# Two layers in one launch: the layer-1 projections without GpSimd products, and half of W_down's products moved behind the last expert pair

## The chip, the cores and the metric

The kernel runs on one core of one Trainium2 chip, in one launch. The metric is the device time of that core in microseconds. TensorE is called PE here, its weight loads PEld, VectorE DVE, ScalarE ACT, GpSimd POOL, and SyncE, which issues most of the transfers, SP.

## The reference

The program computes two transformer layers over 2048 tokens of width 512, all in 32-bit floats. Each layer is: a modulated normalization, attention, a residual sum with a gate, a second modulated normalization, a feed-forward part, and a second residual sum with a gate.

- Layer 0: 16 heads with windows of 64 tokens. Its feed-forward part sends each token to 8 of 64 experts (inner width 192), with weights renormalized over the 8.
- Layer 1: queries, keys and values are projections `x @ Wq + bq`, `x @ Wkv + bkv` (16 query heads, 4 key heads). Queries and keys are rotated by position, `x * cos + rotate_half(x) * sin`. The attention sees 16 first tokens and a window of 128.
- The feed-forward part of layer 1, cut to what matters:

```python
x = fwht(x * SU_ug) / SCALE
x_up = x @ W_up.T * (Wscale_ug[:INTER] * SCALE)
x_gate = x @ W_gate.T * (Wscale_ug[INTER:] * SCALE)
x = jax.nn.silu(x_gate) * x_up
x = fwht(x * SU_dp) / SCALE
x = x @ W_down.T * (Wscale_dp * SCALE)
```

`fwht` is a Walsh-Hadamard transform. The one in front of `W_down` is linear, so the kernel applies it to `W_down` instead of to the activations.

## The kernel before

The tokens lie in 16 tiles of 128 rows, in `x_sb`. The stages follow each other: layer-0 attention with the routing, the expert pairs, the layer-1 projections, the layer-1 attention, the layer-1 feed-forward part.

**Expert pairs** (1019 to 1032 us is the last of them). The 64 experts, sorted by load, are served two at a time, in 32 turns `q`. SP fetches an expert's weights two turns ahead (`fetch_w`, tiles `w1` and `w2`, four buffers each). POOL gathers the token rows and later adds the results `yo` into six arrays `sums[0..5]` in DRAM with indirect transfers; turns from 21 on add into the last three only. From turn 22 on, the first three arrays are loaded back (`earlier`, tiles `sa`) and added to `x_sb` on DVE. After the pairs comes a hardware loop `tc.For_i(0, n_more, 1)` for tokens that found no room; here it runs zero times, but all engines meet before it.

**W_down beside the pairs.** `beside()` is a generator that takes two steps in each turn. For each of four column blocks `cb` it loads a block of `W_down` (`wd_load`, tile `wda`), runs four butterfly steps over it on DVE between `wda` and `wdb` (`wd_step`, L992 and L993), multiplies by the 128x128 Hadamard matrix on PE (`wdh`, four products per block), scales the result from PSUM by `ws_dp` on DVE (L1001), and writes the block to `wd_d` in DRAM. The feed-forward part loads `wd_d` after the attention.

**Layer-1 projections** (1040 to 1199 us). The tiles go in five groups, `GROUPS`, of 2, 2, 4, 4 and 4. `prepare(g)` returns steps and a function `across`. A step is `summed(i)` of one tile and `normal(i - 1)` of the tile before: three sums of `x_sb` with the last three arrays (`rest(i)`, loaded by SP; L1155), statistics, a square root on ACT (L1204), then the normalized tile `xn` on DVE. `across` transposes the `xn` tiles of a group on PE (`nT`, L1220) and writes the scaled `hT`.

While group `g` goes through its five matrices (`c` from -1 to 3: the keys, then four blocks of queries), DVE does one step of group `g + 1` per matrix. For each matrix PE makes eight weight passes. DVE makes `by_sin` from PSUM (sum with the bias, product with sin). ACT makes `by_cos` from PSUM and POOL multiplies it by cos (L1274). PE turns `by_sin` by a permutation matrix (`rot`) and DVE adds `by_cos` to that. Behind the group the value matrix `v` is made, and POOL adds the output bias of the attention, `bo1`, to the group's tiles (L1304); behind group 2 it also scales `wo` (L1307). `v_` and `mm_` issue each instruction behind the one before on its engine; the other instructions are placed by a scheduler that orders each engine's queue.

**Layer-1 attention.** For each tile POOL copies a window of keys (`kw`), PE makes scores, DVE masks them, ACT takes exponents, and PE makes values and the output.

Of the kernel before, what the change touches and what calls it, by code (L numbers as in the profile page):

```python
# [12 lines left out]
F32 = mybir.dt.float32  # L13
# [3 lines left out]
AF = mybir.ActivationFunctionType  # L17
# [111 lines left out]
def block_kernel(ctx: ExitStack, tc: tile.TileContext, t: dict, out: bass.AP):  # L129
# [720 lines left out]


    ex = served.enter_context(tc.tile_pool(name="ex", bufs=4))
    with tc.tile_pool(name="h1", bufs=1) as h1, tc.tile_pool(name="p_x", bufs=2, space=PSUM) as p_x, tc.tile_pool(
        name="p_g", bufs=3, space=PSUM
    ) as p_g, tc.tile_pool(name="p_y", bufs=3, space=PSUM) as p_y:

        def fetch_x(r):
            st_[r]["xg"] = []
# [92 lines left out]
        def earlier(n):  # L951

            got = []
            for i in (2 * n, 2 * n + 1):
                for k in range(3):
                    j, at = divmod(3 * i + k, 4)
                    if at == 0:
                        tag, bufs = ("wdb", 1) if j % 3 == 2 else ("wda", 2)
                        st_["sa"] = h1.tile([P, 4, D], F32, tag=tag, name=f"sa_{j}", bufs=bufs)
                    part = st_["sa"][:, at, :]  # L960
                    nc.sync.dma_start(out=part, in_=sums[k][i * P : (i + 1) * P, :])
                    got.append((i, part))
            return got
# [13 lines left out]
            V.tensor_scalar(ws_dp, ws_dp, 1.0 / math.sqrt(INTER), None, ALU.mult)  # L977

        def wd_load(cb):
            a = h1.tile([P, FC, P], F32, tag="wda", name=f"wda_{cb}", bufs=2)  # L980
            nc.sync.dma_start(out=a, in_=t["L1_Wdown"][cb])
            return a

        def wd_step(cb, a):

            b = h1.tile([P, FC, P], F32, tag="wdb", name=f"wdb_{cb}")
            src, dst = a, b
            h = 1
            while h < FC:
                x = src.rearrange("p (n two h) m -> p n two (h m)", two=2, h=h)  # L990
                y = dst.rearrange("p (n two h) m -> p n two (h m)", two=2, h=h)
                V.tensor_tensor(y[:, :, 0, :], x[:, :, 0, :], x[:, :, 1, :], ALU.add)  # L992
                V.tensor_tensor(y[:, :, 1, :], x[:, :, 0, :], x[:, :, 1, :], ALU.subtract)  # L993
                src, dst = dst, src
                h *= 2
                yield
            for c4 in range(0, FC, 4):
                ps = p_x.tile([P, 4, P], F32, tag="xp", name=f"wdh_{cb}_{c4}")
                with in_turn():
                    st_["pe"] = mm(ps, had, src[:, c4 : c4 + 4, :])  # L1000
                V.tensor_tensor(dst[:, c4 : c4 + 4, :], ps, bc(ws_dp[:, cb * P : (cb + 1) * P], 1, 4), ALU.mult)  # L1001
                if c4 == 4:
                    yield
            nc.sync.dma_start(out=wd_d[cb], in_=dst)
# [13 lines left out]
                yield  # L1018

        side = beside()  # L1020
        NQ = len(ROOM)

        def turn(q):

            steps = []
            for r in (2 * q, 2 * q + 1):
                st_[r]["xT"], chunk = x_T(r, st_[r]["xg"], ROOM[q])
                steps += [lambda f=chunk, c=c: f(c) for c in range(KC)]
            return steps
# [23 lines left out]
        for q in range(NQ):  # L1053
            if q == NQ - 1:
                n_more = nc.values_load(more[0:1, 0:1], min_val=0, max_val=MORE)
            two = [st_[2 * q], st_[2 * q + 1]]
            late = st_.pop("late", [])
            if LATE < q <= LATE + NT // 2:
                st_["late"] = earlier(q - LATE - 1)

            def fetch(p):
                for r in (2 * p, 2 * p + 1) if p < NQ else ():
                    fetch_w(r)
                    fetch_x(r)

            if q:
                fetch(q + 2)
            steps = turn(q + 1) if q + 1 < NQ else []
            with in_turn():
                hA, hB, last = gate_up(  # L1070
                    q, [s["w"][0] for s in two], [s["xT"] for s in two], ROOM[q], lambda: take(steps, 2),
                    lambda: take(opening, KC),
                )
            if q == 0:
                fetch(2)
            take(steps, 2)
            if q + 1 < NQ:
                with tc.issue_after(last.ins):
                    shares(q + 1)
            for s in range(0, ROOM[q], P):  # L1080

                with in_turn(), tc.issue_after(st_["gx"].ins):
                    down(q, s, [a["w"][1] for a in two], hA, hB, ROOM[q], [a["share"] for a in two], to_sums(q))
                take(steps, 2)
            take(steps, 2 * KC)
            with tc.issue_after(last.ins):
                for _ in range(2):
                    next(side)
                for i, part in late:
                    V.tensor_tensor(x_sb[:, i, :], x_sb[:, i, :], part, ALU.add)  # L1090


        with tc.For_i(0, n_more, 1) as j:
# [42 lines left out]
    with tc.tile_pool(name="a1", bufs=1) as ap:  # L1136
# [4 lines left out]
        va = ap.tile([P, NT, P], F32, tag="va", name="va")  # L1141
        vs = ap.tile([P, NT, P], F32, tag="vs", name="vs")
        v2 = ap.tile([80, NT, 2, P], F32, tag="v2", name="v2")
        with tc.tile_pool(name="b1", bufs=1) as bp, tc.tile_pool(name="b1h", bufs=2) as hp, tc.tile_pool(
            name="b1n", bufs=5
        ) as np_, tc.tile_pool(name="cb", bufs=3) as cb, tc.tile_pool(name="b1ps", bufs=8, space=PSUM) as psA:

            prev = {}
# [4 lines left out]
            def v_(f, *a):  # L1153
                with after("V"):
                    prev["V"] = f(*a)  # L1155
# [22 lines left out]

            rest(0, nc.scalar)
            rest(1, nc.scalar)  # L1180
            wk = load(bp, "L1_Wk", [P, KC, P])
            wq = load(bp, "L1_Wq", [P, KC, D], nc.scalar)
            angle(0)
            rest(2)
            wv = load(bp, "L1_Wv", [P, KC, P])
            wo = load(ap, "L1_Wo", [P, KC, D])
            hTs = {}

            def prepare(g):
# [17 lines left out]
                def normal(i):  # L1207
                    mv, rs = norms[i]
                    v_(V.reciprocal, rs, rs)
                    xn = np_.tile([P, D], F32, tag="xn", name=f"xn_a1_{i}")  # L1210
                    v_(V.tensor_scalar, xn, x_sb[:, i, :], mv[:, 0, 0:1], rs[:, 0:1], ALU.subtract, ALU.mult)
                    norms[i] = xn

                def across():
# [27 lines left out]
            for step in steps:  # L1242
                step()
            across()
            for g, (first, n) in enumerate(GROUPS):
                w_ = n * P
                cols = slice(first * P, first * P + w_)
                cos, sin = angles[g]
                hT = hTs[g]
                steps, across = [], None  # L1250
                if g + 1 < len(GROUPS):
                    angle(g + 1)
                    steps, across = prepare(g + 1)
                waiting = []

                def turned():
# [7 lines left out]
                for c in range(-1, KC):  # L1264
                    ps = psA.tile([P, D], F32, tag="ps", name=f"q1_{g}_{c}")[:, 0:w_]
                    for k in range(KC):
                        w = wk[:, k, :] if c < 0 else wq[:, k, c * P : (c + 1) * P]
                        mm_(ps, w, hT[:, k, 0:w_], k == 0, k == KC - 1)
                    bias = bk if c < 0 else bq[:, c : c + 1]
                    by_sin = np_.tile([P, D], F32, tag="by_sin", name=f"by_sin_{g}_{c}", bufs=2)[:, 0:w_]  # L1270
                    v_(V.scalar_tensor_tensor, by_sin, ps, bias, sin, ALU.add, ALU.mult)
                    by_cos = np_.tile([P, D], F32, tag="by_cos", name=f"by_cos_{g}_{c}", bufs=3)[:, 0:w_]
                    S.activation(by_cos, ps, AF.Identity, bias=bias)
                    prev["G"] = G.tensor_tensor(by_cos, by_cos, cos, ALU.mult)  # L1274
                    add = turned() if waiting else None
                    if steps:
                        steps.pop(0)()
                    if add:
                        add()
                    waiting.append((c, by_cos, by_sin))  # L1280
# [17 lines left out]
                if g == 0:  # L1298
                    nc.sync.dma_start(
                        out=v2[64:80, :, :, :].rearrange("p i a m -> p (i a) m"), in_=bc(va[0:16, 0, :], 1, 2 * NT)  # L1300
                    )
                with after("G"):
                    for i in range(first, first + n):
                        G.tensor_tensor(x_sb[:, i, :], x_sb[:, i, :], bo1, ALU.add)  # L1304
                    if g == 2:
                        for k in range(KC):
                            G.tensor_tensor(wo[:, k, :], wo[:, k, :], m1[2], ALU.mult)  # L1307


        fx = ctx.enter_context(tc.tile_pool(name="fx", bufs=1, side="right"))  # L1310
        with tc.tile_pool(name="s1", bufs=2) as sp, tc.tile_pool(name="q_s", bufs=4, space=PSUM) as p_s, tc.tile_pool(
# [20 lines left out]
            def scores(i, cp):  # L1332
# [1 line left out]

                nk = P if i == 0 else W + 16
                mask = con(("mask0", "mask1", "mask2")[min(i, 2)])
                if i > 0 and cp == 0:
                    keys[i] = window(i)
                if cp == 0:
                    totals[i] = small.tile([P, 4, 4], F32, tag="tot", name=f"tot_{i}")  # L1340
                for c in (2 * cp, 2 * cp + 1):
# [399 lines left out]
```

## Time and profile before

| what | value |
|---|---|
| median of 3 runs | 2061.43 us (2055.21 to 2065.03) |
| profiled execution, its own time | 2055.3 us |
| its span, first to last instruction | 2053.5 us |
| mean granted clock of TensorE | 0.972 |
| PE busy | 1943.5 us (95%) |
| DVE busy | 1082.3 us (53%) |
| POOL busy | 589.6 us (29%) |
| ACT busy | 511.1 us (25%) |
| last product of the pairs starts, first transpose of layer 1 starts | 1031 us, 1053.4 us |
| first matrix of groups 0, 1, 2, 3, 4 starts | 1055.6, 1076.1, 1102.4, 1137.8, 1172.6 us |
| first scores of the layer-1 attention | 1199.3 us |

Times inside the table's last three rows are counted from the span's start. A share of busy time is an average over stages with different limits, so each stage is read by itself: in the windows of the profile, in the timeline, and in what ended an engine's idle time (given in brackets behind an instruction, as "idle before" and the releaser). Engines name the line of the kernel; where a helper issues the instruction, as at L134 and L1155, the names of the tiles tell what it is.

### The profile page before, as it was taken

To read this page: it belongs to the slowest core of one execution; us is meant where nothing else is said; L and a number is where in the kernel's file an instruction comes from. 1 tells how busy PE (TensorE), PEld (TensorE's weight loads), DVE (VectorE), ACT (ScalarE), POOL (GpSimd) and SP (SyncE) were. 2 spreads that over 40 slices of the span, in tenths; PEclk is the share of its full clock that TensorE was granted. 3 is DMA by queue.
4 is the path that set the end of the run, shared out by engine and by line. 5 is a ranking of instruction groups with operands and counts; after the bars stand their busy time and mean duration, and the time that the engine had idled before them with its cause. 6 is when DMAs were issued, how large, how long until landed. Compare 5 with 4: busy or idle time off the path is not lost. (4 is left out here: it accounts for less than half of the span.)

```text
span 2053.5 us, 28795 instructions
## 1 busy us (share of the span) xinstructions
PE 1943.5 (95%) x10794; PEld 1245.2 (61%) x10794; DVE 1082.3 (53%) x2566; ACT 511.1 (25%) x1190; POOL 589.6 (29%) x463
## 2 busy tenths in 40 slices
PE   8999878999999999999957889999999999999998
PEld 4655545455555556666634555556776777767776
DVE  3566564544444433345548657766545535545443
ACT  2333323111111111111111157774111111111101
POOL 1500003576666766566522420020010010010000
PEclk9999968999999999999979899999999999999999
DMA  7780036688888899999964100002211211211210
GB/s 281 293 329 22 32 113 206 156 213 233 208 233 221 225 245 241 267 319 314 270 195 146 48 12 2 2 23 95 91 62 42 83 44 59 82 42 62 83 41 21
DMA packets 121166, 290.31 MB, mean 141 GB/s; under 512 B 20968, under 2 KB 28904, under 8 KB 118464
## 3 DMA queue, kind: packets, MB, share of 16 engines
q1 hardware_dynamic: 83552, 207.13, 29.3%
q0 software_dynamic: 36032, 77.30, 17.8%
q10 hardware_dynamic: 1440, 4.00, 0.5%
q8 instruction: 87, 1.43, 0.3%
q14 instruction: 55, 0.45, 0.1%
HBM read 209.92 MB, written 76.10 MB: 139 GB/s over the span
## 5 line engine op out<-in xcount | busy, mean ns | idle before, releaser
L934 POOL DMA_INDIRECT sum<-yo,tidx x164 | 269.9, 1646 | 108.8 <-issue 39.2
L608 POOL DMA_INDIRECT xring<-h_d,tidx x164 | 180.4, 1100 | 377.6 <-PE rps L134 232.3
L134 PE MATMUL gu<-xT,w 128*128 128x312 f32 (+26 forms) x1024 | 244.4, 397 | 0.0
L134 PE MATMUL y<-wd,act 128*128 128x512 f32 x512 | 230.3, 593 | 1.5 <-DVE act L1510 1.4
L134 PEld LDWEIGHTS gu<-xT,w 128*128 128x128 f32 x1024 | 190.2, 191 | 54.5 <-issue 17.3
L134 PEld LDWEIGHTS y<-wd,act 128*128 128x128 f32 x512 | 97.0, 190 | 98.0 <-issue 91.4
L876 ACT ACTIVATE xT<-xp,modc,modc 128x312 f32<-128x312 f32 (+26 forms) x128 | 74.2, 580 | 329.5 <-PE xp L873 302.9
L930 DVE SCALAR_TENSOR_TENSOR yo<-y,wc,modr 128x512 f32<-128x512 f32 (+22 forms) x164 | 116.6, 745 | 74.5 <-PE y L134 74.1
L134 PE MATMUL y<-w,hA 128*128 128x512 f32 (+22 forms) x328 | 149.8, 596 | 1.1 <-DVE yo L930 1.0
L237 POOL TENSOR_TENSOR xh<-hT 128x1024 f32<-128x1024 f32 x4 | 9.4, 2359 | 418.0 <-ACT hT L1585 402.8
L896 DVE TENSOR_TENSOR hA<-hA,gu 128x312 f32<-128x312 f32 (+26 forms) x64 | 28.2, 440 | 188.1 <-PE xp L873 107.9
L134 PE MATMUL p<-xt,ws 128*128 128x256 f32 x512 | 122.6, 383 | 3.5 <-DVE ws L1510 3.5
L134 PE MATMUL gub<-xT,w 128*64 128x312 f32 (+26 forms) x1024 | 125.4, 398 | 0.0
L134 PE MATMUL p<-xt,wr 128*128 128x256 f32 x512 | 120.8, 379 | 0.0
L1371 ACT ACTIVATE pr<-ng,nb 128x208 f32<-128x208 f32 (+1 forms) x256 | 115.0, 450 | 22.8 <-DVE nb L1361 22.8
L873 PEld LDWEIGHTS xp<-cst,xring 128*128 128x128 f32 x656 | 73.1, 143 | 73.0 <-issue 57.9
L134 PE MATMUL p<-xh,wr 128*128 128x256 f32 x512 | 116.5, 379 | 0.0
L134 PEld LDWEIGHTS p<-xt,ws 128*128 128x128 f32 x512 | 97.9, 192 | 27.9 <-issue 15.8
L134 PEld LDWEIGHTS p<-xt,wr 128*128 128x128 f32 x512 | 96.8, 190 | 23.6 <-issue 10.8
L873 PE MATMUL xp<-cst,xring 128*128 128x128 f32 x656 | 100.2, 284 | 6.1 <-DMA xring<-h_d,tidx 4.9
L134 PEld LDWEIGHTS p<-xh,wr 128*128 128x128 f32 x512 | 97.0, 190 | 13.6 <-issue 0.7
L1665 ACT ACTIVATE sg<-two,L_ws_gate 128x512 f32<-128x512 f32 x32 | 23.1, 722 | 309.0 <-DVE two L1510 309.0
(378 smaller groups left out, 2992.4 us busy)
## 6 DMA issues: line engine op xcount, KB each, us to landing
w<-in_L_gu SPq DMA_DIRECT2D x64, 768.0 KB, 7.5
wr<-in_L_Wug SPq DMA_DIRECT2D x64, 512.0 KB, 4.5
sum<-xring SPq DMA_DIRECT2D x6, 4352.0 KB, 30.9
w<-in_L_dn SPq DMA_DIRECT2D x64, 256.0 KB, 8.7
sa<-sum SPq DMA_DIRECT2D x48, 256.0 KB, 10.5
sum<-sum SPq DMA_DIRECT2D x44, 256.0 KB, 3.3
w<-in_L_dn SPq DMA_DIRECT2D x64, 128.0 KB, 9.1
xring<-in_L_wmod SPq DMA_DIRECT2D x4, 1536.0 KB, 11.0
```

Source lines behind the costliest of these rows:

```text
L134: return TE.matmul(o, lhsT, rhs, start=start, stop=stop)
L237: eng.tensor_tensor(b[:, :, 0, :], a[:, :, 0, :], a[:, :, 1, :], ALU.add)
L608: return G.indirect_dma_start(out=dst, out_offset=None, in_=src[:, :], in_offset=bass.IndirectOffsetOnAxis(ap=idx, axis=0))
L873: st_["pe"] = TE.transpose(xp[:, b * P : (b + 1) * P], xg[:, c * P : (c + 1) * P], ident)
L876: S.activation(xT[:, c, 0:n], xp[:, 0:n], AF.Identity, bias=sh, scale=sc)
L896: V.tensor_tensor(o[:, 0:n], o[:, 0:n], ps[1][:, 0:n], ALU.mult)
L930: V.scalar_tensor_tensor(yo, ys[h], shares[h][rows, b : b + 1], m0[5][rows, :], ALU.mult, ALU.mult)
L934: G.indirect_dma_start(out=sums[k][:, :], out_offset=bass.IndirectOffsetOnAxis(ap=idx, axis=0), in_=yo, in_offset=None, compute_op=ALU.add,)
L1371: S.activation(prs[i, c][:, j, :nk], ng[:, :nk], AF.Exp, bias=nb, scale=-1.0, accum_out=totals[i][:, c, j : j + 1],)
L1665: S.activation(sg, gate, AF.Silu, scale=wsg[:, f : f + 1])
```

## The change

1. **W_down.** For the column blocks 2 and 3, DVE scales the block by `ws_dp` in SBUF behind the butterflies, and the block goes to `wd_d` without the Hadamard product. In the last turn these blocks are loaded again in eight pieces, into buffers of expert weights (`fetch_last`). Behind the last pair PE makes the eight products, ACT and DVE copy them out by turns, and ACT and SP write them back to `wd_d` (`last_products`).
2. **Weights.** `Wk`, `Wq`, `Wv` and the first group's cos and sin are loaded in the last turn (`load_proj`) into two `wda` buffers, which move to a pool of their own that stays open through the projections.
3. **Projections.** `by_cos` is made by one DVE instruction from PSUM, with the bias and cos, as `by_sin` is. `xn` is made by ACT, with a small `off` from DVE. The bias adds of `x_sb` and the scaling of `wo` stand in the source of the attention now, still on POOL.
4. **Order.** `prepare(g + 2)` is called behind group `g`, and its first step (the sums of the first tile) is done there.

The diff, cut to its core:

```diff
+    h2 = early.enter_context(tc.tile_pool(name="h2", bufs=2, side="right"))
+    def load_proj():
+        a, b = (h2.tile([P, 4 * D], F32, tag="wda", name=f"proj_{i}") for i in range(2))
+        at = 0
+        for key, w, n in (("L1_Wk", b, P), ("L1_Wq", a, D), ("L1_Wv", b, P)):
+            lo = at if w is b else 0
+            proj[key] = w[:, lo : lo + KC * n].rearrange("p (k m) -> p k m", k=KC)
+            nc.sync.dma_start(out=proj[key], in_=t[key])
+            at += KC * n if w is b else 0
+        proj["angle"] = [b[:, at + 2 * P * k : at + 2 * P * (k + 1)] for k in range(2)]
+        for k in range(2):
+            nc.sync.dma_start(out=proj["angle"][k], in_=t["rope"][k][:, 0 : 2 * P])
...
+            if cb >= 2:
+                for c8 in (0, 8):
+                    part = src[:, c8 : c8 + 8, :]
+                    V.tensor_tensor(part, part, bc(ws_dp[:, cb * P : (cb + 1) * P], 1, 8), ALU.mult)
+                    yield
+                nc.sync.dma_start(out=wd_d[cb], in_=src)
+                yield
+                return
...
+        def fetch_last():
+            parts = [(cb, c4) for cb in (2, 3) for c4 in range(0, FC, 4)]
+            got = []
+            for tag, n in (("w1", 3), ("w2", 2), ("w1", 3)):
+                a = ew.tile([P, KC, 2 * FI] if tag == "w1" else [P, 2, D], F32, tag=tag, name=f"wdl_{len(got)}")
+                a = a.rearrange("p k f -> p (k f)").rearrange("p (g c m) -> p g c m", c=4, m=P)
+                for g in range(n):
+                    cb, c4 = parts[len(got)]
+                    nc.sync.dma_start(out=a[:, g], in_=wd_d[cb][:, c4 : c4 + 4, :])
+                    got.append((cb, c4, a[:, g]))
+            return got
+        def last_products(got):
+            for n, (cb, c4, a) in enumerate(got):
+                ps = p_x.tile([P, 4, P], F32, tag="xp", name=f"wdh_{cb}_{c4}")
+                with in_turn():
+                    st_["pe"] = mm(ps, had, a)
+                o = ex.tile([P, D], F32, tag="yo", name=f"wdo_{n}", bufs=8).rearrange("p (c m) -> p c m", c=4)
+                (V.tensor_copy if n % 2 else S.copy)(o, ps)
+                (nc.sync if n % 2 else nc.scalar).dma_start(out=wd_d[cb][:, c4 : c4 + 4, :], in_=o)
...
+            if q == NQ - 1:
+                load_proj()
+                behind_it = fetch_last()
...
+        last_products(behind_it)
         with tc.For_i(0, n_more, 1) as j:
...
+                    off = small.tile([P, 1], F32, tag="off", name=f"off_a1_{i}")
+                    v_(V.scalar_tensor_tensor, off, mv[:, 0, 0:1], -1.0, rs, ALU.mult, ALU.mult)
                     xn = np_.tile([P, D], F32, tag="xn", name=f"xn_a1_{i}")
-                    v_(V.tensor_scalar, xn, x_sb[:, i, :], mv[:, 0, 0:1], rs[:, 0:1], ALU.subtract, ALU.mult)
+                    S.activation(xn, x_sb[:, i, :], AF.Identity, bias=off, scale=rs)
...
-                    S.activation(by_cos, ps, AF.Identity, bias=bias)
-                    prev["G"] = G.tensor_tensor(by_cos, by_cos, cos, ALU.mult)
+                    v_(V.scalar_tensor_tensor, by_cos, ps, bias, cos, ALU.add, ALU.mult)
...
-                with after("G"):
-                    for i in range(first, first + n):
-                        G.tensor_tensor(x_sb[:, i, :], x_sb[:, i, :], bo1, ALU.add)
-                    if g == 2:
-                        for k in range(KC):
-                            G.tensor_tensor(wo[:, k, :], wo[:, k, :], m1[2], ALU.mult)
+                made = [], None
+                if g + 2 < len(GROUPS):
+                    angle(g + 2)
+                    made = prepare(g + 2)
+                    made[0].pop(0)()
...
-                if i > 0 and cp == 0:
-                    keys[i] = window(i)
+                if cp == 0:
+                    if i > 0:
+                        keys[i] = window(i)
+                    G.tensor_tensor(x_sb[:, i, :], x_sb[:, i, :], bo1, ALU.add)
+                    if i == 1:
+                        for k in range(KC):
+                            G.tensor_tensor(wo[:, k, :], wo[:, k, :], m1[2], ALU.mult)
```

More of the change, by code (lines that the diff above doesn't have):

```diff
@@ L852, in block_kernel @@
     ex = served.enter_context(tc.tile_pool(name="ex", bufs=4))
+    early = ExitStack()
+    h2 = early.enter_context(tc.tile_pool(name="h2", bufs=2, side="right"))
+    proj = {}
+    def load_proj():
[9 more added lines that the diff above has]
+            nc.sync.dma_start(out=proj["angle"][k], in_=t["rope"][k][:, 0 : 2 * P])
     with tc.tile_pool(name="h1", bufs=1) as h1, tc.tile_pool(name="p_x", bufs=2, space=PSUM) as p_x, tc.tile_pool(
@@ L855, in block_kernel @@
     ) as p_g, tc.tile_pool(name="p_y", bufs=3, space=PSUM) as p_y:
+        NQ = len(ROOM)
         def fetch_x(r):
@@ L957, in earlier @@
                     if at == 0:
-                        tag, bufs = ("wdb", 1) if j % 3 == 2 else ("wda", 2)
-                        st_["sa"] = h1.tile([P, 4, D], F32, tag=tag, name=f"sa_{j}", bufs=bufs)
+                        pool, tag = (h1, "wdb") if j % 3 == 2 else (h2, "wda")
+                        st_["sa"] = pool.tile([P, 4, D], F32, tag=tag, name=f"sa_{j}")
                     part = st_["sa"][:, at, :]
@@ L979, in wd_load @@
         def wd_load(cb):
-            a = h1.tile([P, FC, P], F32, tag="wda", name=f"wda_{cb}", bufs=2)
+            a = h2.tile([P, FC, P], F32, tag="wda", name=f"wda_{cb}")
             nc.sync.dma_start(out=a, in_=t["L1_Wdown"][cb])
@@ L1020, in block_kernel @@
         side = beside()
-        NQ = len(ROOM)
+        def fetch_last():
[17 more added lines that the diff above has]
+                (nc.sync if n % 2 else nc.scalar).dma_start(out=wd_d[cb][:, c4 : c4 + 4, :], in_=o)
         def turn(q):
@@ L1143, in block_kernel @@
         v2 = ap.tile([80, NT, 2, P], F32, tag="v2", name="v2")
-        with tc.tile_pool(name="b1", bufs=1) as bp, tc.tile_pool(name="b1h", bufs=2) as hp, tc.tile_pool(
-            name="b1n", bufs=5
+        with tc.tile_pool(name="b1h", bufs=2) as hp, tc.tile_pool(
+            name="b1n", bufs=4
         ) as np_, tc.tile_pool(name="cb", bufs=3) as cb, tc.tile_pool(name="b1ps", bufs=8, space=PSUM) as psA:
@@ L1180, in block_kernel @@
             rest(1, nc.scalar)
-            wk = load(bp, "L1_Wk", [P, KC, P])
-            wq = load(bp, "L1_Wq", [P, KC, D], nc.scalar)
-            angle(0)
+            wk, wq, wv = (proj[key] for key in ("L1_Wk", "L1_Wq", "L1_Wv"))
+            angles[0] = proj["angle"]
             rest(2)
-            wv = load(bp, "L1_Wv", [P, KC, P])
             wo = load(ap, "L1_Wo", [P, KC, D])
@@ L1244, in block_kernel @@
             across()
+            angle(1)
+            made = prepare(1)
             for g, (first, n) in enumerate(GROUPS):
@@ L1249, in block_kernel @@
                 hT = hTs[g]
[L1250 to L1253, printed above, removed]
+                steps, across = made
                 waiting = []
@@ L1271, in block_kernel @@
                     v_(V.scalar_tensor_tensor, by_sin, ps, bias, sin, ALU.add, ALU.mult)
-                    by_cos = np_.tile([P, D], F32, tag="by_cos", name=f"by_cos_{g}_{c}", bufs=3)[:, 0:w_]
-                    S.activation(by_cos, ps, AF.Identity, bias=bias)
-                    prev["G"] = G.tensor_tensor(by_cos, by_cos, cos, ALU.mult)
+                    by_cos = np_.tile([P, D], F32, tag="by_cos", name=f"by_cos_{g}_{c}", bufs=2)[:, 0:w_]
+                    v_(V.scalar_tensor_tensor, by_cos, ps, bias, cos, ALU.add, ALU.mult)
                     add = turned() if waiting else None
@@ L1301, in block_kernel @@
                     )
-                with after("G"):
-                    for i in range(first, first + n):
-                        G.tensor_tensor(x_sb[:, i, :], x_sb[:, i, :], bo1, ALU.add)
-                    if g == 2:
-                        for k in range(KC):
-                            G.tensor_tensor(wo[:, k, :], wo[:, k, :], m1[2], ALU.mult)
+                made = [], None
[3 more added lines that the diff above has]
+                    made[0].pop(0)()
+        early.close()
         fx = ctx.enter_context(tc.tile_pool(name="fx", bufs=1, side="right"))
```

## The prediction

> **What bounds the kernel now.** The page's slices first: PE is at nine tenths or more nearly everywhere and dips once, after the expert pairs. The windows say where; columns are window, length, then busy time of PE, PEld, DVE, ACT and POOL, granted clock, DMA share, GB/s.
>
> ```profile
> 1020.00:1030.00 10.00, 10.00 (x66) 6.63 (x64) 1.86 (x5) 0.80 (x3) 3.97 (x3) 1.00 0.48 61
> 1030.00:1040.00 10.00, 2.05 (x7) 0.34 (x6) 2.09 (x3) 0.00 (x0) 6.06 (x4) 0.77 0.61 77
> 1090.00:1100.00 10.00, 4.13 (x18) 3.53 (x19) 8.59 (x20) 2.32 (x5) 4.09 (x4) 0.67 0.61 200
> 1120.00:1130.00 10.00, 4.54 (x13) 1.97 (x12) 9.68 (x19) 1.97 (x4) 1.90 (x2) 0.88 0.49 158
> ```
>
> PE is full up to the last pair, nearly empty from 1032 to 1053, and half idle in the projections exactly where DVE is full. The timeline of one four-tile group says why.
>
> ```profile
> 1116.44 0.74 DVE L1155 SCALAR_TENSOR_TENSOR by_sin<-q,L_bq,sin 128x512 f32<-128x512 f32 x1
> 1117.10 3.08 DVE L1155 TENSOR_TENSOR x_sb<-x_sb,sum 128x512 f32<-128x512 f32 x3
> 1122.26 0.74 DVE L1155 SCALAR_TENSOR_TENSOR by_sin<-q,L_bq,sin 128x512 f32<-128x512 f32 x1
> ...
> 1124.08 0.38 PE L1220 MATMUL nT_a<-cst,xn_a 128*128 128x128 f32 x2
> 1127.62 0.47 PE L1220 MATMUL nT_a<-cst,xn_a 128*128 128x128 f32 x1 [3.16 <-DVE xn_a L1155]
> 1129.54 1.75 PE L1220 MATMUL nT_a<-cst,xn_a 128*128 128x128 f32 x7 [1.44 <-DVE xn_a L1155]
> ```
>
> DVE needs 5.82 us per matrix (1116.44 to 1122.26), PE 4.29 (eight weight passes 3.43, rotation 0.86). So PE reaches the transposes at 1124.1, waits for the last xn until 1129.5, and then does 13 transposes in 3.03 us at the lowered clock. Of the 5.82, 3.08 are three sums beside a GpSimd product; the same three cost 2.11 alone:
>
> ```profile
> 1049.67 2.11 DVE L1155 TENSOR_TENSOR x_sb<-x_sb,sum 128x512 f32<-128x512 f32 x3
> ...
> 1143.01 1.59 POOL L1274 TENSOR_TENSOR by_cos_-1_8993<-by_cos_-1_8993,cos 128x512 f32<-128x512 f32 x1 [2.23 <-ACT by_cos_-1_8993 L1273]
> 1130.92 4.95 POOL L1304 TENSOR_TENSOR x_sb<-x_sb,L_bo 128x512 f32<-128x512 f32 x4
> ```
>
> Last, W_down's products inside the pairs, and the end of the pairs:
>
> ```profile
> 635.53 1.98 PE L134 MATMUL wdh<-wda,cst 128*128 128x512 f32 x4
> 637.94 1.98 PE L134 MATMUL wdh<-wda,cst 128*128 128x512 f32 x4 [0.43 <-DVE wdb L1001]
> 639.76 2.59 PE L134 MATMUL gu<-xT,w 128*128 128x288 f32 x10
> ...
> 1036.01 1.45 POOL L934 DMA_INDIRECT sum<-yo,tidx  x1 [0.57 <-issue]
> 1040.49 0.82 SPq L1167 DMA_DIRECT2D sum<-sum  x2
> ```
>
> The products stand in a PE stream without gaps, so they cost their length. The layer-1 sums start when the last scatter has landed (1036.01 + 3.70 in the chain).
>
> **The change, part by part.**
>
> *Pairs.* Eight products leave PE: 635.53 to 639.76 is 4.23 us, two stretches of 1.82 (from 707.86 and 731.74) make 3.64, together **-7.9**. On DVE eight 0.68 us scalings (5.4) become four 1024-wide ones at the butterflies' 1.22 (4.9): nothing, and DVE is busy 5 to 8 of each 10 us there; if it filled up, PE would wait at the pair's ends. The two new steps per column block end by pair 17, before the sums of pair 22 want the buffers.
>
> *Loads in the last pair.* On SP the Wk and Wv loads now stand before the down weights of expert 62 and all of 63. The built order has Wk wait for the add of sum buffer 9, in pair 29's late adds, done at 998.9; SP issues expert 62 at 1002.2, so no wait. Expert 63 was issued at 1005.9, lands in 7.5 and is wanted near 1021: 7 us to spare against 0.5 MB at about 320 GB/s, 1.6. Wq, rope and eight pieces of W_down follow (3.4 MB, about 11 us), from 1011 on, mostly in the 0.48 DMA window. I take 0; if they ran late, the last products would wait, up to +4.
>
> *Behind the last pair.* Eight products at 0.86 run from 1032 to 1039 into empty PE time; a copy on ACT or DVE (0.6 to 0.7) keeps step with two banks. The price is the barrier before the loop: it waits for the copies' writes too. The seventh product ends at 1038.2, its copy at 1038.9, ACT issues the write by 1039.4, and the fastest loads shown land in 3.1 to 3.3: 1042.5 instead of 1039.9, **+2.5**. Writes of this size beside scatters are not in the trace: below, 0.5 (DVE's eighth copy, 1040.4, ends last); above, the 7.0 us landing of scatters under load, +6. Light load is nearer. The eighth write goes ahead of the first sum load on SP (0.4 of issue).
>
> *Opening.* The first xn go to ACT (0.7 behind 0.15 of DVE, for 0.55): +0.5. Wk, rope and Wq no longer share DMA with the first sums, whose second piece lands only at 1047.3: worth 0 to 1.5. Net **0**, between -1.5 and +1.
>
> *Projections.* Per tile DVE drops xn (0.47 start to start) for the small off (0.15), adds by_cos per matrix at by_sin's 0.64 (128x256: 0.39), and runs the sums beside no product. In a 512 step: by_sin 0.64, by_cos 0.64, sums 2.11, statistics 0.83, reciprocal and off 0.28, rotation add 0.60: 5.1 for 5.8. The first tile's sums being done in the group before, only three steps and a bit remain before the last xn: from the end of the first matrix 4.5 + 5.1 + 5.1 + 1.6 = 16.3, and 0.8 through ACT: 17.1. PE arrives at 17.2. So the wait goes, and with it the slow transposes: 1.9 + values 3.7 + rotation 0.9 + next first matrix 3.4 gives 27.1 per group, 28.5 with the next tile's sums overhanging (0.8) and some contention. The same walk over before (4.55 + 3 x 5.75 + 1.2, then 3.0 + 4.5 + 0.9 + 3.4) gives 34.8 for 35.4 measured. First matrix to first matrix:
> - group 0 (2 tiles): 18.3 for 20.5, as sums take 2.11, not 2.67
> - group 1 (2 tiles, preparing 4): PE waits for xn at 14.5, DVE 1.6 behind: 23.6 for 26.3
> - groups 2 and 3: 28.5 each for 35.4 and 34.8
> - group 4: PE-bound before and after, 26.6
>
> 125.5 for 143.5, less 0.5 for products on Wo: **-17.5**. What is late next is PE itself.
>
> GpSimd is not emptied. The source puts the bias adds and Wo's scaling into attention, but the built order has all 20 on POOL ahead of the first window copy, each bias add waiting only for its tile's xn on ACT. So they run in the projections, no longer bunched: xn is ready 0.9 after off, when DVE turns to the rotation add and the two products from PSUM, about 1.9 us; of POOL's 1.27 some 0.3 reaches into the next sums. Bounds: no overlap, -20; full overlap at the row's 0.97 each for the 12 tiles whose sums are on the path, -6. The order puts it near the first. The Trainium skill (SBUF — State Buffer, § Who interferes with whom) says that a DVE instruction with two SBUF inputs and a GpSimd instruction that reads SBUF exclude each other, the loser blocked for the whole instruction. This speaks against moving adds next to sums; the trace shows 0.97 lost to a product of 1.59. By the rule the full overlap would cost 1.27 each and leave about -2.
>
> *Attention and after.* PE, DVE and ACT keep their order there; POOL's last bias add follows the last xn of group 4, made before that group's own matrices (26.6 us), so the window copies find POOL free: 0.
>
> Sum: -7.9 + 2.5 + 0 - 17.5 = -22.9. The profiled execution (2055.3, span 2053.5) becomes 2032.4. It is 6.1 below the median of the runs, 2061.4, for which the forecast is **2038.5**.
>
> **Rivals.**
> - *DVE stays full in the projections*: the 20 GpSimd instructions meet the sums after all (for it: 3.08 against 2.11; against: the order above). The projections give 2 to 6: the total is -7 to -11, about 2052.
> - *The tail gives the pairs' gain back*: the write-backs and late pieces hold the barrier 8 us longer (for: DMA share above 1.0 up to 1010; against: 0.48 from 1020). About -17: 2044.
> - *Slower*: SP, which issues in order, is stopped at the Wk load. Behind it stand expert 62's down weights and all of 63, so pair 31 stands still. Each us beyond the 7 to spare is added to the time; it eats the 22.9 if the add comes after 1029, as it would if the wait fell on the last pair's own adds. At 1035 it is +6: 2067. Against: the built wait names pair 29, at 998.9.
> - *It doesn't do what it says*: POOL keeps 20 of its 45 instructions here; this is in the sum.
>
> **How the numbers follow.** Forecast 0.72, first rival 0.13, tail 0.08, slower 0.07. A measurement tells about 0.5% (10 us) from no change; faster means below 2051. From the forecast 0.69, the tail 0.07 and the first rival 0.04 make faster 0.80; the rest of these 0.13 within; slower 0.07. The lower bounds together (-7.9 + 0.5 - 1.5 - 20 = -29) end at 2032, and single runs stand up to 6 below their median: low 2027. The high end takes in the first rival and its spread, 2056.
>
> **What would show it.** No wdh row before 1020 but eight behind the last y; SP's first sum load 2 to 3 us later after the last y than before's 8.4; sum triples near 2.1 to 2.4; four-tile groups 28 to 29 apart and their transposes near 1.9, not 3.0; bias adds on POOL one by one; attention's length unchanged. It is wrong if sum triples stay near 3, if PE still waits for xn over 3 us in groups 2 and 3, if gu rows of pair 31 wait, or if the barrier comes more than 6 us later.

## The result and the profile after

The changed kernel takes **2044.48 us** (median of 11 runs, 2033.98 to 2053.81), the kernel before beside it 2060.95 (median of 11): a ratio of 0.9921, with a 95% interval of 0.9905 to 0.9938, or 16.3 us (12.8 to 19.6) less. The profiled execution took 2033.98 us (span 2032.2); it was the fastest of the eleven, and 21.3 us of span lie between it and the profiled execution of before. Where these 21.3 lie:

| stretch | before | after | forecast |
|---|---|---|---|
| start to the end of the last `y` | 1032.0 | 1023.8 (-8.3) | -7.9 |
| last `y` to the first sum load (the tail) | 8.4 | 14.1 (+5.7) | +2.5 |
| first sum load to the first K matrix (the opening) | 15.1 | 13.4 (-1.7) | 0 |
| first K matrix to the first scores (the projections) | 143.7 | 129.4 (-14.3) | -17.5 |
| attention (to PE's first `p<-xt`), then the rest | 227.8, 626.4 | 226.3, 625.3 (-2.6) | 0 |

Groups 0 to 4 take 19.1, 26.5, 28.3, 28.8 and 26.7 us (forecast 18.3, 23.6, 28.5, 28.5, 26.6). The windows of the changed kernel, columns as before:

```profile
1020.00:1030.00 10.00, 10.00 (x26) 2.83 (x24) 4.74 (x7) 1.76 (x3) 6.06 (x4) 1.00 0.95 215
1080.00:1090.00 10.00, 5.86 (x18) 4.16 (x17) 9.66 (x21) 2.00 (x4) 2.50 (x3) 0.83 0.62 217
1110.00:1120.00 10.00, 8.99 (x28) 4.11 (x27) 9.72 (x22) 2.81 (x5) 3.28 (x3) 1.00 0.49 157
```

In group 2 (third line) PE and DVE are now both nearly full. In group 1 (second line) DVE is still full, PE is not, and the granted clock is down to 0.83. Around the end of the last pair (first line; the last `y` ends at 1023.8) the DMA share is 0.95; before it was 0.48 from 1020 and 0.61 from 1030. The timeline of the same four-tile group, DVE and PE:

```profile
1111.25 0.74 DVE L1211 SCALAR_TENSOR_TENSOR by_sin<-q,L_bq,sin 128x512 f32<-128x512 f32 x1
1112.57 2.37 DVE L1211 TENSOR_TENSOR x_sb<-x_sb,sum 128x512 f32<-128x512 f32 x3
1116.64 0.74 DVE L1211 SCALAR_TENSOR_TENSOR by_sin<-q,L_bq,sin 128x512 f32<-128x512 f32 x1
...
1118.40 0.49 PE L1277 MATMUL nT_a<-cst,xn_a 128*128 128x128 f32 x3
1119.24 1.64 PE L1277 MATMUL nT_a<-cst,xn_a 128*128 128x128 f32 x13 [0.35 <-ACT xn_a L1268]
```

A step of DVE takes 5.39 us for 5.82, the three sums 2.37 for 3.08, and the transposes run right behind the last matrix, 13 in 1.64 us for 3.03. What PE waits for in all projections (us in total, times, longest) tells the same: for `xn` it waited 13.3 us before.

```profile
PE rot L134 <- DVE by_sin L1211: 9.4, 7, 2.9
PE nT_a L1277 <- ACT xn_a L1268: 2.2, 4, 1.3
```

Between the pairs and the first sum stands a chain that was not there before. From the chain of waits (start, length):

```profile
1025.69 5.35 DMA sum<-yo,tidx
...
1031.14 0.59 ACT wdo L1070
...
1031.75 3.16 DMA wd_d<-wdo
...
1035.64 2.22 DMA wd_d<-wdo
1037.88 0.36 ACTq L1223
```

A scatter lands; then ACT copies the seventh product; then its write lands, and the engines meet before the loop; then the eighth write lands, and only then do SP and ACT issue the first sum loads.

### The profile page after: what moved, and what is told of

It reads as the page before. It is cut to its first block, busy times and chain, and to the rows that moved or that the text cites. A ratio compares the mean times of both kernels' runs of the same rounds, so it can differ in the third digit from the quotient of the medians.

```text
span 2032.2 us, 28791 instructions
## 1 busy us (share of the span) xinstructions
PE 1936.8 (95%) x10794; PEld 1237.7 (61%) x10794; DVE 1087.7 (54%) x2591; ACT 509.8 (25%) x1185; POOL 563.7 (28%) x438
## 4 chain that ended last, share of the span: by engine, by line
PE 77%; DVE 8%; DMA 5%; ACT 5%; issue 1%; POOL 0%; SPq 0%; ACTq 0%; DVEq 0%; POOLq 0%
PE y L134 20%; PE p L134 18%; PE gu L134 11%; PE gub L134 5%; PE xp L893 4%; PE s L134 3%; ACT pr L1431 3%; PE po L134 2%; PE po_a L134 2%; DMA w<-in_L_gu 2%; PE pt L1376 2%; DVE x_sb L1211 1%; DMA sum<-yo,tidx 1%; PE tps L134 1%; PE o L134 1%
## 5 line engine op out<-in xcount | busy, mean ns | idle before, releaser
L134 PEld LDWEIGHTS gu<-xT,w 128*128 128x128 f32 x1024 | 189.8, 191 | 58.0 <-issue 18.3
L134 PEld LDWEIGHTS p<-xt,wr 128*128 128x128 f32 x512 | 96.8, 190 | 23.6 <-issue 10.8
L134 PEld LDWEIGHTS p<-xh,wr 128*128 128x128 f32 x512 | 96.9, 190 | 14.3 <-DVE u L1570 0.7
## 6 DMA issues: line engine op xcount, KB each, us to landing
w<-in_L_dn SPq DMA_DIRECT2D x64, 128.0 KB, 8.9
```

The lines of the kernel that those rows point to most:

```text
L134: return TE.matmul(o, lhsT, rhs, start=start, stop=stop)
```

## The experiments

Each ratio is against the kernel before, run beside it; the unchanged parts of a kernel are those of the changed one unless its text says otherwise. Four kernels went in each of three sets; the kernel before had medians of 2060.0, 2067.5 and 2066.4 in them, so kernels of different sets are compared by their ratios.

**The two parts alone** (`w_alone`: projections as before, with two buffers for `by_cos` instead of three; `p_alone`: W_down as before).

> The changed kernel with the projections as before (xn on VectorE, the cosine product on ScalarE and GpSimd, sums in the group's own steps, GpSimd's adds behind each group); W_down's products, their copies and the loads in the last pair stay as in the change. Theory (the parts add as the two traces show them: the last y ends 8.3 us sooner, 1023.7 for 1032.0; the first sum load stands 14.2 us behind it instead of 8.4; the first K matrix 13.4 behind the load instead of 15.1): 4 us faster than before, projections 143.7 from the first K matrix to the first scores as before. Rival (the medians, which moved by 16.5 where the two profiled executions differ by 21.3, fall short because the pairs do not keep their 8.3 us): no gain or a loss of up to 2, with the last y near 1030.

> The kernel before with the projections of the change alone (xn on ScalarE, the cosine product on VectorE, the first tile's sums a group ahead, GpSimd's adds tile by tile); W_down's products stay in the pairs and the weights load behind the last pair as before. Theory: first K matrix to first scores 129 us instead of 143.7, opening 0.5 longer, so 14 us faster than before. Rival (the projections are faster only because their weights were loaded early): 135 or more, 8 faster. If the parts add, this and the W_down part alone sum to the whole change's 16 to 21.

`w_alone` 1.000 (0.9983 to 1.0017): nothing. Its last `y` ends at 1026.6, 5.5 sooner; its first sum load stands 15.6 behind it, 7.2 more than before; the opening is 2.1 shorter; the projections take 144.0. Here the pairs kept most of their gain and the stretch behind them took it all, so neither the 4 us of the theory nor its rival's cause is right. The same chain, longer:

```profile
1028.63 5.90 DMA sum<-yo,tidx
...
1035.25 3.92 DMA wd_d<-wdo
...
1039.89 2.30 DMA wd_d<-wdo
```

`p_alone` 0.9939 (0.9917 to 0.9960), 12.6 us faster, projections 129.4 as in the whole change, so they are not short because their weights were loaded early. The gain is the projections' part; the 4 us by which the whole change is ahead of it lie within the intervals.

**What the tail waits for.**

```diff
-                o = ex.tile([P, D], F32, tag="yo", name=f"wdo_{n}", bufs=8).rearrange(...)
-                (V.tensor_copy if n % 2 else S.copy)(o, ps)
-                (nc.sync if n % 2 else nc.scalar).dma_start(out=wd_d[cb][:, c4 : c4 + 4, :], in_=o)
+                (V.tensor_copy if n % 2 else S.copy)(a, ps)
+                (nc.sync if n % 2 else nc.scalar).dma_start(out=wd_d[cb][:, c4 : c4 + 4, :], in_=a)
```

> The changed kernel with each of the eight last products copied over its own operand instead of into a buffer of the yo ring. Theory (in the changed kernel's chain the copy of the seventh product waits for a scatter that still reads its buffer, 1025.69 to 1031.06, and the first sum load waits for the landing of the eighth write, 1035.64 to 1037.88): the eighth landing gates nothing any more, -2.2, and the copies follow the products, -0.5 to -1; first sum load 10.5 to 11.5 behind the last y instead of 14.2, 3 us faster than the changed kernel. Rival (the write-backs themselves set the barrier, wherever they start from): under 1 us.

Ratio 0.9917 (0.9894 to 0.9939), the changed kernel's. The two waits are gone from the chain, and the first sum load stands 12.8 behind the last `y` (14.1 to 16.1 in the others of this order). That is more than the 10.5 to 11.5 of the theory, for the seventh write landed in 4.46 us here and not in 3.16. And the opening takes 15.0 instead of 13.0 to 14.0, so the first K matrix is 27.8 behind the last `y`: no gain, as the rival said. The theory had the waits right and their worth wrong.

**The products behind the loop** (`behind`: operands overwritten as above, writes from GpSimd's queue; `best`: with `hold` below; `best2`: and the first two tiles' loads all from SP).

```diff
-        last_products(behind_it)
         with tc.For_i(0, n_more, 1) as j:
             ...
+        st_.pop("pe")
+        last_products(behind_it)
```

> The changed kernel with the eight last products placed behind the leftover loop instead of ahead of it, each copied over its own operand and written from GpSimd's queue. Theory (W_down's part is worth nothing because its copies and writes stand ahead of the barrier that the first sums wait for; first sum load 14.1, 15.7 and 16.1 us behind the last y in three executions with the change's order, 8.2 and 8.4 in two without the products): first sum load 8 to 9 behind the last y, the products then run while the sums are loaded, first K matrix 15 to 16 behind that load as it was before, 24 in all for 27.5 to 29: 4 us faster than the changed kernel. Rival (the empty time behind the pairs is bound by the DMA engines, whatever the order): the writes delay the sums by as much, under 1 us.

> The last products behind the loop, as in the run of that, and GpSimd's 20 instructions held for the values of group 3, as in the run of that. Theory (the two costs are independent): 7 us from the one and 4 from the other, 11 us faster than the changed kernel and about 28 faster than the kernel before, with projections of 122 us and 24 from the last y to the first K matrix. Rival: as the held kernel, 24 faster than before, if the barrier's share comes back in the opening.

> The last products behind the loop, GpSimd held, and the first two tiles' sums loaded from SP's queue alone. Theory (with the products behind the loop the first K matrix still came 28.0 us behind the last y, because the sum loads issued by ScalarE stand behind its copies, which wait for TensorE: 1041.31, 1043.98, 1047.04, 1048.84): all six loads go out in 2.5 us, the first K matrix comes 24 to 25 behind the last y, 3 to 4 us faster than the held kernel, 27 faster than before (0.987). Rival (the writes of the products take the DMA engines from the sums): 27 or more, no gain over the held kernel (0.9886).

`behind` 0.9915 (0.9894 to 0.9936), level with the changed kernel: the first sum load is back at 8.3 behind the last `y`, but the first K matrix is 28.0 behind it. ACT's sum loads stood in its queue behind copies that waited for PE:

```profile
1043.98 0.34 ACTq L1222 DMA_DIRECT2D sum<-sum  x1
1047.04 0.59 ACT L1069 COPY wdl<-wdh 128x512 f32<-128x512 f32 x1 [2.48 <-PE wdh L134]
1047.04 0.82 ACTq L1222 DMA_DIRECT2D sum<-sum  x2
```

`best2` takes the loads out of that queue, and then the first sum stands on DVE behind two copies, issued at 1052.1 and 1054.8 as PE delivers them: 29.4 from the last `y` to the first K matrix, ratio 0.9886 (0.9865 to 0.9906). `best` 0.9887 (0.9866 to 0.9908) with 27.6, as its rival said. Behind the loop PE also comes to the products after 9 to 11 us of idleness and at a lower granted clock: they take 9.8 us in `behind` (clock 0.82 from 1043 to 1053) and 10.3 in `best2` (0.70 from 1048 to 1058), for 7.7 in the changed kernel. Without W_down's products behind the pairs this stretch is 23.6 to 24.6 (before, `p_alone`, `p_hold`); with them it was 27.5 to 30.1, wherever they stood. Whether the writes take DMA time from the sums was not separated from the order of the queues and from this slower PE.

**GpSimd's adds beside the sums.** In the changed kernel's group 1, DVE and POOL:

```profile
1079.05 3.08 DVE L1211 TENSOR_TENSOR x_sb<-x_sb,sum 128x512 f32<-128x512 f32 x3
1084.35 3.16 DVE L1211 TENSOR_TENSOR x_sb<-x_sb,sum 128x512 f32<-128x512 f32 x3
...
1079.27 1.58 POOL L1395 TENSOR_TENSOR x_sb<-x_sb,L_bo 128x512 f32<-128x512 f32 x1 [11.10 <-ACT xn_a L1268]
1084.24 1.27 POOL L1395 TENSOR_TENSOR x_sb<-x_sb,L_bo 128x512 f32<-128x512 f32 x1 [3.39 <-ACT xn_a L1268]
```

Each add begins when ACT has made its tile's `xn`; in group 1 DVE is in the next sums by then, or enters them 0.1 us later. `hold` makes POOL wait, by data:

```diff
+                    if i == 0:
+                        zero = small.tile([P, 1], F32, tag="zero", name="zero")
+                        G.tensor_scalar(zero, va[:, 11, P - 1 : P], 0.0, None, ALU.mult)
+                        for w in (bo1, m1[2]):
+                            G.tensor_tensor(w[:, 0:1], w[:, 0:1], zero, ALU.add)
                     G.tensor_tensor(x_sb[:, i, :], x_sb[:, i, :], bo1, ALU.add)
```

> The changed kernel with GpSimd's 20 additions and scalings made to wait for the values of group 3 (a zero taken from them is added to one element of the bias and of the gate), so that they run beside group 4, where VectorE makes no sums. Theory (GpSimd's adds cost the sums: triples of 3.62, 3.08, 3.16 and 2.96 us beside them, 2.13 alone): every triple at 2.1 to 2.2, group 1 from 26.5 us to 23.5 with its transposes near 1.7 instead of 3.0, group 0 19.1 to 18.0, groups 2 and 3 down by 0.5 to 1 each: 5 to 6 us faster than the changed kernel. Rival (group 1 is bound by VectorE's own work and the triples are long for another reason): under 1 us. Against it: the 20 take 25 us from 1155 on, so the first window copies, wanted at 1187, may come late by up to 2.

> The projections' part alone (W_down's products in the pairs, weights loaded behind them, as before) with GpSimd's 20 instructions held for the values of group 3. Theory (W_down's part is worth nothing, holding is worth 7): 20 us faster than before, level with the changed kernel with GpSimd held (0.9886) within 4 us; projections 122, last y to first K matrix 24.5. Rival (W_down's part is worth its 8 us of products where the projections are short): 8 us slower than that, 0.9925.

`hold` 0.9886 (0.9863 to 0.9910), 23.5 us faster than before and some 7 faster than the changed kernel. Every triple (the three sums of one tile) in the projections takes 2.13 or 2.14, the groups 18.1, 22.3, 27.2, 27.7 and 26.7, the projections 122.0. The attention takes 227.0 for 226.3: the 20 instructions end at 1175.8, and the first scores start at 1175.7.

```profile
1080.52 2.13 DVE L1211 TENSOR_TENSOR x_sb<-x_sb,sum 128x512 f32<-128x512 f32 x3
...
1151.28 2.49 POOL L1400 TENSOR_TENSOR x_sb<-x_sb,L_bo 128x512 f32<-128x512 f32 x2
```

`p_hold` 0.9906 (0.9889 to 0.9923), projections 122.6. Against `best` and `best2` (0.9887, 0.9886) or `hold`, W_down's part is worth 0.2%, 4 us, with intervals that overlap: nothing is not excluded, and the rival's 8 us lies at the edge of what they allow.

**Which edit of the projections brings it.** Each run takes one back (`late_sums`: `prepare(g + 1)` inside the group, as before; `cos_back`: the two lines of `by_cos` as before; `xn_back`: the line of `xn` as before), beside the changed kernel itself (`again`).

> The changed kernel without the sums a step sooner: each group's preparation begins behind its own first matrix, as before; the cosine product stays on VectorE, xn on ScalarE, GpSimd's adds tile by tile. Theory (VectorE, with four steps of 5.1 to 5.4 us before the last xn instead of three and a bit, becomes the later engine again): about 3 us more in each of groups 1 to 3, and transposes near 3.0 us instead of 1.6 in groups 2 and 3: 8 to 11 us slower than the changed kernel. Rival (moving the work off VectorE made the room, the order does nothing): under 2 us.

> The changed kernel with the cosine product back on ScalarE and GpSimd (two buffers); sums a step sooner, xn on ScalarE, GpSimd's adds tile by tile. Theory (what counts is that GpSimd's products stand beside the sums): triples near 3.0 again, so VectorE gives 0.64 a matrix and gets 0.9 back; groups 1 to 3 longer by 1 to 2 each, 3 to 5 us slower than the changed kernel. Rival (what counts is VectorE's own work): 0.64 less a step, 1 to 3 us faster.

> The changed kernel with xn back on VectorE (one 0.47 instead of the 0.15 of the offset and a ScalarE activation). Theory (each step of VectorE grows by 0.3, but the path to the transposes loses 0.7 of ScalarE; GpSimd's add follows VectorE's xn and meets the next sums in full, triples near 3.1): projections 129.4 to 133, 1 to 4 us slower than the changed kernel. Rival (xn on ScalarE is what made the room): more than 5 us slower.

> The changed kernel itself, for a second profiled execution and as the base of this set. Theory (the first profiled execution was lucky in what stands ahead of the projections: its first sum load 14.1 us behind the last y where four others of the same order had 15.5 to 16.1): first sum load about 15.5 to 16 behind the last y, first K matrix 28 to 30 behind it, projections 129.4 again within 0.5; 0.8% faster than the kernel before. Rival (the first execution is typical): 27.5 from the last y to the first K matrix.

| kernel | ratio | projections | groups 1, 2, 3 |
|---|---|---|---|
| `again` | 0.9935 (0.9912 to 0.9958) | 127.6 | 25.1, 28.3, 28.8 |
| `late_sums` | 0.9988 (0.9974 to 1.0003) | 146.5 | 29.1, 35.2, 34.7 |
| `cos_back` | 0.9942 (0.9921 to 0.9964) | 134.1 | 24.2, 30.0, 32.1 |
| `xn_back` | 0.9902 (0.9885 to 0.9919) | 128.0 | 25.2, 27.9, 28.4 |

Without the sums a step sooner nothing is left of the gain, though GpSimd's products are gone; 11 to 14 us by the ratios, more than the 8 to 11 expected, and the projections are 2.8 longer than before. PE then waits for `xn` in the projections for longer than before (13.3):

```profile
PE nT_a L1277 <- ACT xn_a L1268: 16.6, 6, 4.6
```

`cos_back` bears out its theory in groups 2 and 3 (group 1 is shorter; the projections are 4.7 to 6.4 longer, and as a ratio the loss is within the intervals): its sums meet an add and a product of POOL.

```profile
1121.17 4.03 DVE L1211 TENSOR_TENSOR x_sb<-x_sb,sum 128x512 f32<-128x512 f32 x3
...
1121.53 1.45 POOL L1396 TENSOR_TENSOR x_sb<-x_sb,L_bo 128x512 f32<-128x512 f32 x1 [2.67 <-ACT xn_a L1268]
1122.94 1.71 POOL L1330 TENSOR_TENSOR by_cos<-by_cos,cos 128x512 f32<-128x512 f32 x1
```

Still, with the cosine product back on ACT and POOL the projections are 9.6 shorter than before (134.1 for 143.7): most of their gain doesn't need that edit.

`xn_back` is a miss for both theories: not slower. With `xn` made on DVE, POOL's add starts 1.16 us ahead of DVE's next sums, not 0.31, and mostly meets the two products from PSUM instead:

```profile
1111.34 1.29 POOL L1393 TENSOR_TENSOR x_sb<-x_sb,L_bo 128x512 f32<-128x512 f32 x1 [12.89 <-DVE xn_a L1211]
...
1112.50 2.14 DVE L1211 TENSOR_TENSOR x_sb<-x_sb,sum 128x512 f32<-128x512 f32 x3
```

So ACT's `xn` saves DVE 0.3 a step and loses as much by making the add late. That `xn_back` has the better ratio is not explained by the projections (128.0 for 127.6); in their two profiled executions the difference stands ahead of them, where the kernels are alike (last `y` at 1028.7 and 1033.8).

`again` had the first sum load 15.0 and the first K matrix 28.6 behind the last `y`: the first execution (27.5) was a lucky one there, as its theory said. But its projections took 127.6, not 129.4 within 0.5: group 1 took 25.1 for 26.5, on account of the clock (last section).

## Why the prediction was right, and where not

The time lay in the range and the direction was right, but the forecast was 6 us too low: 22.9 us were forecast, 16.3 came. The 21.3 of the two profiles are closer to it by luck: the tail and the projections missed by 3.2 each, and the opening, the attention and the rest, held at nothing, gave 4.3 of that back in this execution. Step by step:

- **Pairs, -7.9.** -8.3 between the two first profiles. With the products moved, the last `y` ended 7.6 us sooner in these and the first set (mean of four profiles, against two), 4.6 in the third (three against one). One wait was not in the sum: in all eleven profiles with the products moved PE waits 1.0 to 3.5 us for `gu` weights, near 880 and 970 us; in the three without, 0, 0 and 4.4 (`p_alone`). As it comes without the move too, it is not shown that the move causes it.
- **Loads in the last pair, 0.** Right: in the changed kernel no `gu` row of the last pair waits for weights, and SP waited 0.2 us for the add in front of Wk. One reading was wrong without effect: the 7.5 us in which expert 63 "lands" is the median of all 64 loads; its own took 12.3 before, which leaves 3 us to spare, not 7.
- **Behind the last pair, +2.5.** The mis-sized term: +5.7 in the first profile, +6.6 to +7.7 in six others of this order, beyond the bound of 6, which the prediction had named as a sign of being wrong. The prediction let the copies follow the products; but their `wdo` buffers belong to the `yo` ring, and the seventh copy waited for a scatter (landing in 5.35 to 6.18 us, not the 3.70 of before): it ended 8.0 us behind the last `y` in the first profile, for the 6.9 of the sum. And it gave the eighth write "0.4 of issue", when the first sum loads, into space that the ring had held, waited 2.2 to 2.3 us for it to land. `tail` shows that both waits are real, and that taking them away does not bring the time back.
- **Opening, 0.** -1.7, and -1.1 to -2.1 in the others of this order: about the -1.5 of the bound.
- **Projections, -17.5.** -14.3. The walk itself was right: with POOL out of the way the projections take 122.0, 21.7 less than before, where it gave 20 for no overlap. The failed step is "of POOL's 1.27 some 0.3 reaches into the next sums". In groups 2 and 3 the triples lose 0.83 and 0.24, in group 1 0.95 and 1.03, and Wo's two products cost the first triple of group 0 1.5 (3.62). The order was read rightly (all 20 in the projections, each add behind its `xn`), but timed for a 512-wide step with a rotation add in it, whose gap from `off` to the next sums is about 1.9; it is 1.3 in the first such step of a group, which has no rotation add, and 0.8 to 1.1 in 256-wide steps. Group 1 alone missed by 2.9, and 1.4 of that is not the overlap but the clock: in `again` the same group took 25.1 (last section). The bound of -6 was summed wrongly as well: it adds the full overlap to a sum that already held a part of it; from the -20 without overlap it comes to -8.
- **Attention, 0.** Right: the stage took 225.8 to 228.9 us in all profiles, 227.8 before and 226.3 after.

Of the rivals, "DVE stays full" did not happen. "The tail gives the pairs' gain back" did, in its mechanism: `w_alone` shows the W_down part at nothing. That the median came to lie at its 2044 is partly luck, for it left the projections at -17.5. It had 0.08; its evidence against, a DMA share of 0.48 from 1020 on, was a row of the kernel before, and the change itself puts its loads and writes there (0.95). The slower one did not either (0.2 us at the Wk load). That GpSimd keeps its 20 instructions was "in the sum"; `hold` prices it at 7 us. One of the signs was worded too widely: the other eight `wdh` products stay inside the pairs, at 457 to 562 us.

The rule that was weighed prices an overlap well. Group 2 has an add that starts 0.31 us ahead of the sums:

```profile
1106.28 1.26 POOL L1395 TENSOR_TENSOR x_sb<-x_sb,L_bo 128x512 f32<-128x512 f32 x1 [13.18 <-ACT xn_a L1268]
1106.59 2.96 DVE L1211 TENSOR_TENSOR x_sb<-x_sb,sum 128x512 f32<-128x512 f32 x3
```

Against 2.13, the triples behind such an add lost 1.03, 0.83 and 0.24 us where 1.16, 0.95 and 0.36 of it lay inside them: all but some 0.13 of the overlap. The Trainium skill (SBUF — State Buffer, § Who interferes with whom) says that the two exclude each other, and the traces agree to that 0.13. It was the overlap that I had wrong, not its price.

The best kernels measured are `hold`, `best` and `best2`, at 0.9886 to 0.9887. `hold` is the least edit. Not tried were GpSimd held and `xn` on DVE together, and the sums a step sooner alone, with both `by_cos` and `xn` as before.

## What to carry to other kernels

Work moved off a crowded engine, or out of its neighbour's way, can bring nothing while the step that waits for it starts as late as before: here nothing of the gain was left without the earlier sums (`late_sums`), and most of it stayed without the cosine edit (`cos_back`). When instructions move to the edge of a barrier, list the buffers that they write and who last read them, for a ring that is free in the steady state is full of pending transfers at its end. And ask of a helper engine's instruction not only how long it is but what the neighbour does when its input is ready; hold it by data, if the source's place does not.

## What was not expected of the hardware

- When DVE's triple was first and POOL's add came into it, both paid: the triple 0.95 over 2.13, the add 1.58 for 1.27.
- Groups 2 to 4 of the changed kernel repeat to 0.1 us. Of the 11.7 us between the spans of its two profiled executions, 10.0 lie ahead of the last `y`.
- The clock differs between executions at one place of one program: behind the same 1.3 us wait in group 1, the 13 transposes took 3.01 us in the first execution of the changed kernel (granted clock 0.79 in 1088 to 1096) and 1.64 in `again` (1.00 in 1098 to 1106). That is 1.4 us without any difference in the code. Two other kernels with these projections, `tail` and `p_alone`, took 3.04 and 1.64 there; what decides it stays open. The rows of the first execution and of `again`:

```profile
1091.81 3.01 PE L1277 MATMUL nT_a<-cst,xn_a 128*128 128x128 f32 x13 [1.31 <-ACT xn_a L1268]
...
1102.58 1.64 PE L1277 MATMUL nT_a<-cst,xn_a 128*128 128x128 f32 x13 [1.31 <-ACT xn_a L1268]
```
